# First stage of a four-layer kernel: context values for 128 tokens at a time, by way of DRAM

## The chip, the cores and the metric

The kernel runs on one core of one Trainium2 chip, as one program. The metric is the time of one execution in device microseconds; a kernel's time is the median of several runs. Five engines work side by side, each through its own queue in order: TensorE (PE; its weight loads are shown as PEld), VectorE (DVE), ScalarE (ACT), GpSimd (POOL) and SyncE (SP), which here issues most DMAs.

## What is computed

The input is x (16 batches of 256 tokens, 256 wide) and a context of 16 x 77 tokens, 256 wide. Four layers add to x in turn, each scaled by the tanh of a gate: an attention of x over context and x together, a mixture of experts, a second cross-attention, a gated linear attention. Only the first one is touched:

```python
x = layer_norm(image_embeds, ln1_g, ln1_b)      # the context, 77 tokens a batch
l = layer_norm(latents, ln2_g, ln2_b)           # the latents (x, normed once before), 256 tokens a batch
q = l @ Wq                                      # 16 heads of 64
kv = jnp.concatenate([x, l], axis=1) @ Wkv      # 333 tokens a batch
k, v = jnp.split(kv, 2, axis=-1)
w = softmax(q k^T / 8)                          # per head, 256 x 333
out = (w v) @ Wo
```

## The kernel before

Everything is float32; in the records each matmul appears as two. The whole first stage is `stage0_fast`. Its engines run in the order in which the code names their instructions (`Pinned`, line 50, so nearly all records bear L50). The work is cut into 64 units, one for each batch b and group g of four heads. A unit runs, on TensorE: the scores of (b, g), then denominators and outputs of the unit before it (`values`), then at g = 1 the transposes of the next batch (`turn`) and the projection of the last one, at g = 2 the values of the next batch (`all_values`), and then queries and keys of the next unit (`heads`).

A batch has 256 tokens of its own and 77 of its context, 333 together. `turn` transposes xn (256 tokens) and cn (77 tokens) into one PSUM pair; VectorE scales them into kvT (128 partitions x 2 x 333), the context behind the tokens. `all_values` cuts the 333 columns into three chunks of KC = 111, and makes values for each chunk with 2 halves of 512 x 2 steps of contraction. ACT copies one half of the result into v, VectorE the other. `heads` makes q (256 columns) and k (333 columns) for two heads at a time; ACT scales q, VectorE copies k.

`scores` has six slots of 111 keys (two pairs of heads x three chunks) by two heads x 256 queries, in three PSUM pairs; ACT takes the exponential of each pair into e. `sums` adds the three chunks on GpSimd into es, and es into esum (a check on the size of the sums). `values` turns es into denominators by a matmul with ones, and e with v into outputs; in the last unit it takes the denominators straight from e (`last`). es and e have two buffers each, oT and cn one. The PSUM pool has four pairs of banks.

Context rows are loaded two batches ahead by SP (`load_c`, line 110), three buffers of 77 rows. At n = 1 SP issues `clear_rows`, 16 writes of 640 KB that clear the experts' rows in DRAM; before them stand all loads of weights and of x.

Of the kernel before, what the change touches and what calls it, by code (L numbers as in the profile page):

```python
# [10 lines left out]
F32 = mybir.dt.float32  # L11
# [6 lines left out]
P = 128  # L18
# [55 lines left out]
def layers(ctx: ExitStack, tc: tile.TileContext, t, out, check):  # L74
# [30 lines left out]
    w12 = s12.enter_context(tc.tile_pool(name="s12w", bufs=1, side="right"))  # L105
    ws1 = s1.enter_context(tc.tile_pool(name="s1w", bufs=1, side="right"))
    if fast:
        ctxs = s0.enter_context(tc.tile_pool(name="f0c", bufs=3))

    def load_c(b):  # L110
        cs[b] = ctxs.tile([S2, D], F32, tag="c", name="c")
        nc.sync.dma_start(out=cs[b], in_=t["ctx"][b])

    vec = const("vec", [P, V_N])
    nc.sync.dma_start(out=vec, in_=t["vec"])
# [16 lines left out]
    nc.sync.dma_start(out=prio, in_=t["prio"])  # L132
    wq2, wk2, wv2, wo2 = (load_w(n, D, D, w12) for n in ("wq2", "wk2", "wv2", "wo2"))
    if fast:
        both, own, pmask = (w12.tile(shape, F32, tag=n, name=n) for n, shape in (
            ("both", [P, 2, D]), ("own", [P, 2, 32]), ("pmask", [P, 2])))
        before, offs = (ws1.tile(shape, F32, tag=n, name=n) for n, shape in (
            ("before", [P, P]), ("offs", [P, 2, 2, 8])))

        gbo = const("gbo", [P, D])  # L140
        for n, x in (("both", both), ("own", own), ("pmask", pmask), ("before", before),
                     ("offs", offs)):
# [390 lines left out]
    def stage0_fast():  # L533
        with ExitStack() as sx:
# [5 lines left out]
            def pair(name):  # L540
                return pairs.tile([P, 2, 512], F32, tag="ps", name=name)
# [3 lines left out]

            esum, rsum = check["esum"], check["rsum0"]

            xn, cn, kvT, v, oT = {}, {}, {}, {}, {}

            y, mvs, tallies = {}, {}, []  # L550

            def norm_c(b):
                mvs[b, "c"] = moments(cs[b].unsqueeze(1), S2, 1)

            def norm_x(b):
                mvs[b, "x"] = moments(xs[b])
# [7 lines left out]

            def normed_all(b):
                xn[b] = w1.tile([P, 2, D], F32, tag="xn", name="xn")
                cn[b] = w1.tile([S2, 1, D], F32, tag="cn", name="cn")
                normed(xn[b], y.pop(b), *mvs.pop((b, "y")))
                normed(cn[b], cs[b].unsqueeze(1), *mvs.pop((b, "c")), S2, 1)

            def turn(b):
                kvT[b] = w2.tile([P, 2, NK], F32, tag="kvT", name="kvT")
                both = pair("tr")
                for k in range(2):
                    ps = both[:, k, :]
                    for i in range(2):
                        pe.transpose(ps[:, i * P:(i + 1) * P], xn[b][:, i, k * P:(k + 1) * P], ident)
                    pe.transpose(ps[:, S:NK], cn[b][:, 0, k * P:(k + 1) * P], ident[:S2, :S2])
                for k in range(2):
                    ps = both[:, k, :]  # L580
                    dve.tensor_scalar(kvT[b][:, k, :S], ps[:, :S], vec[:, V_LN2G + k:V_LN2G + k + 1],
                                            vec[:, V_LN2B + k:V_LN2B + k + 1], ALU.mult, ALU.add)
                    dve.tensor_scalar(kvT[b][:, k, S:], ps[:, S:NK], vec[:, V_LN1G + k:V_LN1G + k + 1],
                                            vec[:, V_LN1B + k:V_LN1B + k + 1], ALU.mult, ALU.add)

            def all_values(b, *between):
                v[b] = w2.tile([KC, 3, 1024], F32, tag="v", name="v")
                for c in range(3):
                    both = pair("v")
                    for h in range(2):  # L590
                        ps = both[:, h, :]
                        for k in range(2):
                            pe.matmul(ps[:KC, :], kvT[b][:, k, c * KC:(c + 1) * KC],
                                             wkv0[:, k, 1024 + h * 512:1024 + (h + 1) * 512],
                                             start=k == 0, stop=k == 1)
                    act.copy(v[b][:, c, :512], both[:KC, 0, :])
                    dve.tensor_copy(v[b][:, c, 512:], both[:KC, 1, :])
                    for x in between[c:c + 1]:
                        x()

            qk = {}

# [14 lines left out]
            def scores(b, g):  # L617

                x_qk = qk.pop((b, g))
                e = w2.tile([KC, 6, 2, S], F32, tag="e", name="e")  # L620
                for u in range(0, 6, 2):
                    sc = pair("sc").rearrange("p j (x s) -> p j x s", x=2)
                    for x in range(2):
                        n, c = divmod(u + x, 3)
                        for j in range(2):
                            r = slice(64 * j, 64 * j + 64)
                            pe.matmul(sc[:KC, j, x, :], x_qk[r, n, S + c * KC:S + (c + 1) * KC],
                                             x_qk[r, n, :S], start=True, stop=True)
                    act.activation(e[:, u:u + 2], sc[:KC].rearrange("p j x s -> p x j s"), AF.Exp)
                return b, g, e  # L630

            def sums(b, g, e):
                es = w2.tile([KC, 2, 2 * S], F32, tag="es", name="es")
                by_chunk = e.rearrange("p (n c) j s -> p n c (j s)", n=2)
                pool.tensor_tensor(es, by_chunk[:, :, 0], by_chunk[:, :, 1], ALU.add)
                pool.tensor_tensor(es, es, by_chunk[:, :, 2], ALU.add)
                for n in range(2):
                    pool.tensor_tensor(esum[:KC], esum[:KC], es[:, n, :], ALU.add)
                return b, g, e, es

            def values(b, g, e, es, last=False):
# [7 lines left out]
                for c in range(3 if last else 1):  # L649
                    for h, r in heads:  # L650
                        n, j = divmod(h, 2)
                        x = e[:, 3 * n + c, j, :] if last else es[:, n, j * S:(j + 1) * S]
                        pe.matmul(den[r, :S], ones[:KC, :32], x, start=c == 0, stop=not last or c == 2)
                for i in range(2):
                    for c in range(3):
                        for h, r in heads:
                            n, j = divmod(h, 2)
                            lo = (4 * g + h) * 64 + 32 * i
                            pe.matmul(ps[r, i * S:(i + 1) * S], v[b][:, c, lo:lo + 32], e[:, 3 * n + c, j, :],
                                      start=c == 0, stop=c == 2)  # L660
# [52 lines left out]
            for n, (b, g) in enumerate(units):  # L713
# [16 lines left out]
                    clear_rows()  # L730
                now = sums(*now)
                if behind is not None:
                    values(*behind)
                if g == 1 and b + 1 < B:
                    turn(b + 1)
                if g == 1 and b > 0:
# [15 lines left out]

            run(ahead_of, B, 0)
            run(behind_scores, B, 0)
            values(*behind, last=True)
            tally()
            run(ahead_of, B, 1)
            run(behind_scores, B, 1)
# [241 lines left out]
    def stage1_fast(keep, prep, bank):  # L1000
        with ExitStack() as sx:
# [6 lines left out]
            def own_bank(name):  # L1008
                return psx.tile([P, 512], F32, tag="ps", name=name)

            dve.tensor_scalar(gbo, both[:, 1, :], gate[:, 2:3], None, ALU.mult)
# [40 lines left out]
            def context(b):  # L1052

                if b % 4 == 0:
                    context_keys(b // 4)
                ps, cT = bank("v"), cTs[b // 4][:, :, b % 4, :]
                for k in range(2):
                    pe.matmul(ps[:S2, :D], cT[:, k, :], wv2[:, k, :], start=k == 0, stop=k == 1)
                vc = keep.tile([S2, D], F32, tag=f"vc{b}", name=f"vc{b}")
                dve.tensor_tensor(vc, ps[:S2, :D], both[:S2, 0, :], ALU.add)  # L1060
                ctx_side[b] = negs[b], kds[b // 4][:, :, :, b % 4 * S2:(b % 4 + 1) * S2], vc


# [960 lines left out]
def _arrays(i):  # L2024
# [4 lines left out]
    def cols(v):  # L2029
# [31 lines left out]
        "both": np.broadcast_to(np.stack([f["L1_xattn_wv_b"], f["L1_xattn_wo_b"]]), (P, 2, D)),  # L2061
# [29 lines left out]
```

## Time and profile before

| | |
|---|---|
| three runs | 1917.66, 1918.72, 1922.24 us; median 1918.72 |
| the profiled execution | 1917.57 us, span 1915.7 us, granted clock 0.995 |
| TensorE, 112 to 966 us (first stage) | busy 852.77 of 854.00 |
| VectorE, ScalarE, GpSimd there | 433.17, 350.90, 517.56 |
| DMA there | 3% of the 16 DMA engines' time, 10 GB/s |
| values, TensorE records | 384 of 128x512, weights 128*111 |
| copies of values | ACT 48 x 586 ns, VectorE 48 x 691 ns |
| exponentials | 192 x 1021 ns |
| GpSimd sums | 64 x 2363, 64 x 2351, 128 x 1274 ns |

A row of the profile names the engine, the operation, output<-inputs by the program's names, and the shapes; 128*111 means 128 rows of contraction and 111 columns of weights. "Idle before" is the engine's idle time before the instruction and what ended it. Matmul durations overlap, so the spacing of a series is read from the chain or from the start times.

### The profile page before, as it was taken

The numbers are of one execution on the slowest core, as the hardware profiler recorded it, in microseconds if no ns is written. First come the engines' busy times: TensorE is split into PE (matmuls) and PEld (weight loads), VectorE is DVE, ScalarE is ACT, GpSimd is POOL, SyncE is SP. The second block draws the span as 40 slices with busy tenths as digits, with TensorE's granted clock in tenths as the row PEclk, the third lists the DMA queues.
The fourth block names the chain that finished last, engine by engine and source line by source line (L and its number), as shares of the span: only waits on it lengthen the run. The fifth ranks groups of instructions, "written<-read, shape, count | busy, mean of one in ns | idle before, by whom it ended". The sixth has DMA issues, their size and how long they took to land.

```text
span 1915.7 us, 34858 instructions
## 1 busy us (share of the span) xinstructions
PE 1886.3 (98%) x13960; PEld 1311.6 (68%) x13960; DVE 1096.9 (57%) x2667; ACT 871.1 (45%) x1790; POOL 991.6 (52%) x891
## 2 busy tenths in 40 slices
PE   8999999999999999999999899999999999999997
PEld 5666666666666666666787766667777777777775
DVE  3334555455554555545464388876666666666654
ACT  3333344343343433434343478744444444454452
POOL 3644756557565575655634656314444444444433
PEclk9999999999999999999999999999999999999999
DMA  9400000000000000000068823000000000000000
GB/s 332 148 1 3 14 11 14 7 11 14 11 14 7 11 14 9 12 7 9 12 220 253 224 43 49 15 1 7 6 7 7 6 12 7 6 7 7 12 7 14
DMA packets 54107, 75.16 MB, mean 39 GB/s; under 512 B 10112, under 2 KB 43760, under 8 KB 53424
## 3 DMA queue, kind: packets, MB, share of 16 engines
q1 hardware_dynamic: 41648, 56.05, 8.7%
q0 software_dynamic: 12288, 16.79, 4.3%
q8 instruction: 112, 1.84, 0.4%
q14 instruction: 59, 0.48, 0.1%
HBM read 39.27 MB, written 33.55 MB: 38 GB/s over the span
## 4 chain that ended last, share of the span: by engine, by line
PE 95%; DVE 2%; ACT 1%; POOL 0%; DMA 0%; issue 0%; SPq 0%; ACTq 0%; POOLq 0%; DVEq 0%
PE o L50 13%; PE qk L50 13%; PE sc L50 10%; PE v L50 9%; PE proj L50 7%; PE kq L1548 6%; PE sc L1548 5%; PE ex L50 3%; PE gq L1548 3%; PE v L1548 3%; PE proj L1548 3%; PE o L1548 3%; PE gz L1548 2%; PE den L1548 2%; PE low L1548 1%; PE ms L1548 1%
## 5 line engine op out<-in xcount | busy, mean ns | idle before, releaser
L50 POOL TENSOR_SCALAR rs<-mv 128x2 f32<-128x2 f32 (+1 forms) x91 | 17.5, 192 | 458.7 <-DVE mv L50 455.1
L50 ACT ACTIVATE qk<-qk 128x256 f32<-128x256 f32 x128 | 49.3, 385 | 343.6 <-PE qk L50 343.5
L50 ACT ACTIVATE e<-sc 111x1024 f32<-111x1024 f32 x192 | 182.3, 1021 | 16.9 <-PE sc L50 16.9
L50 PE MATMUL sc<-qk 64*111 64x256 f32 x1536 | 182.2, 383 | 0.0
L50 PE MATMUL o<-e,v 111*32 111x256 f32 x3072 | 177.5, 379 | 0.0
L50 PE MATMUL v<-wkv,kvT 128*111 128x512 f32 x384 | 169.1, 597 | 0.6 <-DVE kvT L50 0.6
L50 DVE RECIPROCAL rd<-o 128x256 f32<-128x256 f32 x64 | 112.3, 1755 | 99.7 <-PE o L50 99.7
L50 PEld LDWEIGHTS sc<-qk 64*111 64x111 f32 x1536 | 132.1, 172 | 52.9 <-issue 29.0
L50 POOL TENSOR_TENSOR esum<-esum,es 111x512 f32<-111x512 f32 x128 | 163.1, 1274 | 10.0
L50 PE MATMUL qk<-kvT,wkv 128*128 128x333 f32 x512 | 164.3, 443 | 0.0
L50 POOL TENSOR_TENSOR es<-e 111x1024 f32<-111x1024 f32 x64 | 151.2, 2363 | 23.9 <-ACT e L50 22.7
L50 POOL TENSOR_TENSOR es<-es,e 111x1024 f32<-111x1024 f32 x64 | 150.4, 2351 | 5.0
L50 PEld LDWEIGHTS o<-e,v 111*32 111x32 f32 x3072 | 99.8, 110 | 66.0
L50 POOL TENSOR_TENSOR k<-e,ee 128x256 f32<-128x256 f32 x64 | 46.8, 731 | 189.4 <-ACT e L50 189.4
L50 DVE COPY qk<-qk 128x333 f32<-128x333 f32 x128 | 64.5, 504 | 124.5 <-ACT qk L50 123.0
L50 PE MATMUL qk<-kvT,wq 128*128 128x256 f32 x512 | 134.3, 385 | 0.0
L50 PEld LDWEIGHTS v<-wkv,kvT 128*111 128x111 f32 x384 | 67.0, 177 | 91.3 <-issue 89.9
L50 POOL TENSOR_TENSOR at<-at,at 128x768 f32<-128x768 f32 x63 | 113.9, 1807 | 24.4 <-DVE at L50 24.4
L50 DVE TENSOR_TENSOR at<-sc,amask 128x768 f32<-128x768 f32 x64 | 61.3, 957 | 113.8 <-PE sc L1548 110.2
L50 POOL DMA_INDIRECT x<-rows_out,pos x64 | 100.4, 1568 | 36.5 <-issue 15.7
L50 PEld LDWEIGHTS qk<-kvT,wkv 128*128 128x128 f32 x512 | 97.2, 190 | 30.0
L50 PEld LDWEIGHTS qk<-kvT,wq 128*128 128x128 f32 x512 | 94.3, 189 | 34.0 <-issue 13.2
(247 smaller groups left out, 4113.7 us busy)
## 6 DMA issues: line engine op xcount, KB each, us to landing
rows<-zero SPq DMA_DIRECT2D x16, 640.0 KB
xin<-rows SPq DMA_DIRECT2D x16, 640.0 KB
rows_out<-y SPq DMA_DIRECT2D x16, 384.0 KB
x<-in_x_dram SPq DMA_DIRECT2D x16, 256.0 KB
rows_out<-y SPq DMA_DIRECT2D x16, 256.0 KB
out_dram<-x SPq DMA_DIRECT2D x15, 256.0 KB
wkv<-in_wkv_dram SPq DMA_DIRECT2D x2, 1024.0 KB
ew<-in_ew_dram SPq DMA_DIRECT2D x2, 1024.0 KB
```

The lines of the kernel that those rows point to most:

```text
L50: x = getattr(self.engine, name)(*a, **k)
L1548: tc.keep_in_program_order(nc.tensor.matmul(*a, **k))
```

## The change

The 16 x 77 = 1232 context tokens are taken as one list and cut into ten groups of 128 (the last of 80). Each group is loaded, normed and transposed once, at the batch in which it begins (batches 0, 1, 3, 4, 6, 8, 9, 11, 13, 14). Its transposes go to a tile ctxT, from which ACT copies each batch's columns into kvT. Its values are made once, copied to a tile vc, and written to one DRAM tile for each batch (vctx); each batch from 1 on reads its 77 rows back into the third chunk of v. Batch 0 gets its rows from PSUM directly. A batch's own tokens give two chunks of 128 values.

The slots of a unit are therefore 128, 128 and 77 keys. The scores go through PSUM in the order (0, 1), (2, 5), (3, 4), so that the two context slots share a pair. es has one buffer. esum takes all 128 partitions. The denominators of the first unit, too, are taken straight from e. The two biases of the third layer come as two tiles (bv, and gbo directly) in place of one (both). Keys are still made for 333 columns in each batch.

```diff
-        ctxs = s0.enter_context(tc.tile_pool(name="f0c", bufs=3))
+        ctxs = s0.enter_context(tc.tile_pool(name="f0c", bufs=2))
+    c_rows = B * S2
+    c_new = {b: j for j in range(-(-c_rows // P)) for b in [P * j // S2]}
+    def c_count(j):
+        return min(P, c_rows - P * j)
+    def c_pieces(b):
+        lo, hi = b * S2, (b + 1) * S2
+        return [(j, max(lo, P * j) - P * j, max(lo, P * j) - lo, min(hi, P * j + P) - max(lo, P * j))
+                for j in range(lo // P, (hi - 1) // P + 1)]
...
             def turn(b):
...
-                    pe.transpose(ps[:, S:NK], cn[b][:, 0, k * P:(k + 1) * P], ident[:S2, :S2])
+                    if n:
+                        pe.transpose(ps[:, S:S + n], cn[b][:n, 0, k * P:(k + 1) * P], ident[:n, :n])
...
-                    dve.tensor_scalar(kvT[b][:, k, S:], ps[:, S:NK], ...)
+                    if n:
+                        dve.tensor_scalar(ctxT[j][:, k, :n], ps[:, S:S + n], ...)
+                for j, at, to, n in c_pieces(b):
+                    act.copy(kvT[b][:, :, S + to:S + to + n], ctxT[j][:, :, at:at + n])
+            def some_values(x, n):
+                both = pair("v")
+                for h in range(2):
+                    for k in range(2):
+                        pe.matmul(both[:n, h, :], x[:, k, :], wkv0[:, k, 1024 + h * 512:1024 + (h + 1) * 512],
+                                         start=k == 0, stop=k == 1)
+                return both
+            def copied(to, both, n):
+                act.copy(to[:n, :512], both[:n, 0, :])
+                dve.tensor_copy(to[:n, 512:], both[:n, 1, :])
             def all_values(b, *between):
...
+                if b in c_new:
+                    j = c_new[b]
+                    n = c_count(j)
+                    both = some_values(ctxT[j][:, :, :n], n)
+                    vc = w1.tile([P, 1024], F32, tag="vc", name="vc")
+                    copied(vc, both, n)
+                    if b == 0:
+                        copied(v[b][:, 2, :], both, S2)
+                    for to in range(1, B):
+                        for jj, at, row, n in c_pieces(to):
+                            if jj == j:
+                                nc.sync.dma_start(out=vctx[to][row:row + n], in_=vc[at:at + n, :])
+                if b > 0:
+                    nc.sync.dma_start(out=v[b][:S2, 2, :], in_=vctx[b])
+                for c in range(2):
+                    copied(v[b][:, c, :], some_values(kvT[b][:, :, chunks[c]], P), P)
+                    if between:
+                        between.pop(0)()
+                for x in between:
+                    x()
...
-                for u in range(0, 6, 2):
+                for slot in ((0, 1), (2, 5), (3, 4)):
...
-                es = w2.tile([KC, 2, 2 * S], F32, tag="es", name="es")
+                es = w1.tile([P, 2, 2 * S], F32, tag="es", name="es")
...
-                pool.tensor_tensor(es, es, by_chunk[:, :, 2], ALU.add)
+                pool.tensor_tensor(es[:S2], es[:S2], by_chunk[:S2, :, 2], ALU.add)
...
-                    values(*behind)
+                    values(*behind, by_chunk=n == 1)
```

More of the change, by code (lines that the diff above doesn't have):

```diff
@@ L107, in layers @@
     if fast:
-        ctxs = s0.enter_context(tc.tile_pool(name="f0c", bufs=3))
+        ctxs = s0.enter_context(tc.tile_pool(name="f0c", bufs=2))
[7 more added lines that the diff above has]
+                for j in range(lo // P, (hi - 1) // P + 1)]
     def load_c(b):
-        cs[b] = ctxs.tile([S2, D], F32, tag="c", name="c")
-        nc.sync.dma_start(out=cs[b], in_=t["ctx"][b])
+        if b in c_new:
+            j, n = c_new[b], c_count(c_new[b])
+            cs[b] = ctxs.tile([P, D], F32, tag="c", name="c")
+            nc.sync.dma_start(out=cs[b][:n], in_=t["ctx"].rearrange("b s d -> (b s) d")[P * j:P * j + n])
     vec = const("vec", [P, V_N])
@@ L134, in layers @@
     if fast:
-        both, own, pmask = (w12.tile(shape, F32, tag=n, name=n) for n, shape in (
-            ("both", [P, 2, D]), ("own", [P, 2, 32]), ("pmask", [P, 2])))
+        bv, own, pmask = (w12.tile(shape, F32, tag=n, name=n) for n, shape in (
+            ("bv", [P, D]), ("own", [P, 2, 32]), ("pmask", [P, 2])))
         before, offs = (ws1.tile(shape, F32, tag=n, name=n) for n, shape in (
@@ L140, in layers @@
         gbo = const("gbo", [P, D])
-        for n, x in (("both", both), ("own", own), ("pmask", pmask), ("before", before),
+        for n, x in (("bv", bv), ("bo", gbo), ("own", own), ("pmask", pmask), ("before", before),
                      ("offs", offs)):
@@ L546, in stage0_fast @@
             esum, rsum = check["esum"], check["rsum0"]
-            xn, cn, kvT, v, oT = {}, {}, {}, {}, {}
+            xn, cn, kvT, v, oT, ctxT = {}, {}, {}, {}, {}, {}
+            vctx = [tc.dram_tile([S2, 1024], F32, name=f"vctx{b}") for b in range(B)]
+            chunks = [slice(0, P), slice(P, S), slice(S, NK)]
+            counts = [P, P, S2]
             y, mvs, tallies = {}, {}, []
             def norm_c(b):
-                mvs[b, "c"] = moments(cs[b].unsqueeze(1), S2, 1)
+                if b in c_new:
+                    n = c_count(c_new[b])
+                    mvs[b, "c"] = moments(cs[b][:n].unsqueeze(1), n, 1)
             def norm_x(b):
@@ L566, in normed_all @@
                 xn[b] = w1.tile([P, 2, D], F32, tag="xn", name="xn")
-                cn[b] = w1.tile([S2, 1, D], F32, tag="cn", name="cn")
                 normed(xn[b], y.pop(b), *mvs.pop((b, "y")))
-                normed(cn[b], cs[b].unsqueeze(1), *mvs.pop((b, "c")), S2, 1)
+                if b in c_new:
+                    n = c_count(c_new[b])
+                    cn[b] = w1.tile([P, 1, D], F32, tag="cn", name="cn")
+                    normed(cn[b][:n], cs[b][:n].unsqueeze(1), *mvs.pop((b, "c")), n, 1)
             def turn(b):
@@ L573, in turn @@
                 both = pair("tr")
+                j = c_new.get(b)
+                n = 0 if j is None else c_count(j)
                 for k in range(2):
@@ L577, in turn @@
                         pe.transpose(ps[:, i * P:(i + 1) * P], xn[b][:, i, k * P:(k + 1) * P], ident)
-                    pe.transpose(ps[:, S:NK], cn[b][:, 0, k * P:(k + 1) * P], ident[:S2, :S2])
+                    if n:
+                        pe.transpose(ps[:, S:S + n], cn[b][:n, 0, k * P:(k + 1) * P], ident[:n, :n])
+                if n:
+                    ctxT[j] = w2.tile([P, 2, P], F32, tag="ctxT", name="ctxT")
                 for k in range(2):
@@ L582, in turn @@
                                             vec[:, V_LN2B + k:V_LN2B + k + 1], ALU.mult, ALU.add)
-                    dve.tensor_scalar(kvT[b][:, k, S:], ps[:, S:NK], vec[:, V_LN1G + k:V_LN1G + k + 1],
-                                            vec[:, V_LN1B + k:V_LN1B + k + 1], ALU.mult, ALU.add)
-            def all_values(b, *between):
[L587 to L599, printed above, removed]
+                    if n:
+                        dve.tensor_scalar(ctxT[j][:, k, :n], ps[:, S:S + n], vec[:, V_LN1G + k:V_LN1G + k + 1],
+                                                vec[:, V_LN1B + k:V_LN1B + k + 1], ALU.mult, ALU.add)
@@ new lines, in all_values @@
+            def all_values(b, *between):
+                v[b] = w2.tile([P, 3, 1024], F32, tag="v", name="v")
+                between = list(between)
+                if b in c_new:
+                    j = c_new[b]
[17 more added lines that the diff above has]
+                    x()
@@ L619, in scores, with values @@
                 x_qk = qk.pop((b, g))
-                e = w2.tile([KC, 6, 2, S], F32, tag="e", name="e")
-                for u in range(0, 6, 2):
+                e = w2.tile([P, 6, 2, S], F32, tag="e", name="e")
+                for slot in ((0, 1), (2, 5), (3, 4)):
                     sc = pair("sc").rearrange("p j (x s) -> p j x s", x=2)
-                    for x in range(2):
-                        n, c = divmod(u + x, 3)
+                    rows = counts[slot[0] % 3]
+                    for x, u in enumerate(slot):
+                        n, c = divmod(u, 3)
                         for j in range(2):
                             r = slice(64 * j, 64 * j + 64)
-                            pe.matmul(sc[:KC, j, x, :], x_qk[r, n, S + c * KC:S + (c + 1) * KC],
+                            pe.matmul(sc[:rows, j, x, :], x_qk[r, n, S + chunks[c].start:S + chunks[c].stop],
                                              x_qk[r, n, :S], start=True, stop=True)
-                    act.activation(e[:, u:u + 2], sc[:KC].rearrange("p j x s -> p x j s"), AF.Exp)
+                    act.activation(e[:rows, slot[0]:slot[1] + 1:slot[1] - slot[0]],
+                                   sc[:rows].rearrange("p j x s -> p x j s"), AF.Exp)
                 return b, g, e
             def sums(b, g, e):
-                es = w2.tile([KC, 2, 2 * S], F32, tag="es", name="es")
+                es = w1.tile([P, 2, 2 * S], F32, tag="es", name="es")
                 by_chunk = e.rearrange("p (n c) j s -> p n c (j s)", n=2)
                 pool.tensor_tensor(es, by_chunk[:, :, 0], by_chunk[:, :, 1], ALU.add)
-                pool.tensor_tensor(es, es, by_chunk[:, :, 2], ALU.add)
+                pool.tensor_tensor(es[:S2], es[:S2], by_chunk[:S2, :, 2], ALU.add)
                 for n in range(2):
-                    pool.tensor_tensor(esum[:KC], esum[:KC], es[:, n, :], ALU.add)
+                    pool.tensor_tensor(esum, esum, es[:, n, :], ALU.add)
                 return b, g, e, es
-            def values(b, g, e, es, last=False):
+            def values(b, g, e, es, by_chunk=False):
                 if g == 0:
@@ L647, in values @@
                 heads = [(h, slice(32 * h, 32 * h + 32)) for h in range(4)]
-                for c in range(3 if last else 1):
+                for c in range(3 if by_chunk else 1):
                     for h, r in heads:
                         n, j = divmod(h, 2)
-                        x = e[:, 3 * n + c, j, :] if last else es[:, n, j * S:(j + 1) * S]
-                        pe.matmul(den[r, :S], ones[:KC, :32], x, start=c == 0, stop=not last or c == 2)
+                        rows = counts[c]
+                        x = e[:rows, 3 * n + c, j, :] if by_chunk else es[:, n, j * S:(j + 1) * S]
+                        pe.matmul(den[r, :S], ones[:rows, :32], x, start=c == 0, stop=not by_chunk or c == 2)
                 for i in range(2):
@@ L658, in values @@
                             lo = (4 * g + h) * 64 + 32 * i
-                            pe.matmul(ps[r, i * S:(i + 1) * S], v[b][:, c, lo:lo + 32], e[:, 3 * n + c, j, :],
+                            rows = counts[c]
+                            pe.matmul(ps[r, i * S:(i + 1) * S], v[b][:rows, c, lo:lo + 32], e[:rows, 3 * n + c, j, :],
                                       start=c == 0, stop=c == 2)
@@ L754, in stage0_fast @@
             run(behind_scores, B, 0)
-            values(*behind, last=True)
+            values(*behind, by_chunk=True)
             tally()
@@ L1009, in own_bank @@
                 return psx.tile([P, 512], F32, tag="ps", name=name)
-            dve.tensor_scalar(gbo, both[:, 1, :], gate[:, 2:3], None, ALU.mult)
+            dve.tensor_scalar(gbo, gbo, gate[:, 2:3], None, ALU.mult)
             kb = w1.tile([P, 2, 2], F32, tag="kb", name="kb")
@@ L1059, in context @@
                 vc = keep.tile([S2, D], F32, tag=f"vc{b}", name=f"vc{b}")
-                dve.tensor_tensor(vc, ps[:S2, :D], both[:S2, 0, :], ALU.add)
+                dve.tensor_tensor(vc, ps[:S2, :D], bv[:S2], ALU.add)
                 ctx_side[b] = negs[b], kds[b // 4][:, :, :, b % 4 * S2:(b % 4 + 1) * S2], vc
@@ L2060, in _arrays @@
         "own": np.broadcast_to(own, (P, 2, 32)).astype(np.float32),
-        "both": np.broadcast_to(np.stack([f["L1_xattn_wv_b"], f["L1_xattn_wo_b"]]), (P, 2, D)),
+        "bv": np.broadcast_to(f["L1_xattn_wv_b"], (P, D)), "bo": np.broadcast_to(f["L1_xattn_wo_b"], (P, D)),
         "x": f["x"], "ctx": f["ctx_1024"], "fside": f["fside_BxSxS2_0"], "mask": f["mask_BxSxS2_ik1"], "vec": vec,
```

## The prediction

> **What bounds the kernel now.** I read the page's busy rows and its chain first, then the chain of waits of one batch of the first stage, then the weight loads, and last the few places where the change adds a wait.
>
> ```profile
> PE 1886.3 (98%) x13960; PEld 1311.6 (68%) x13960; DVE 1096.9 (57%) x2667; ACT 871.1 (45%) x1790; POOL 991.6 (52%) x891
> PE 95%; DVE 2%; ACT 1%; POOL 0%; DMA 0%; issue 0%; SPq 0%; ACTq 0%; POOLq 0%; DVEq 0%
> ```
>
> TensorE is busy 98% of the span and 95% of the chain that ended last; in the first stage from 112 to 966 us it is busy 852.77 of 854.00. So a matmul less there is time less, unless another engine then falls behind. The chain in order of time (start, us, what) for the batch from 472 us:
>
> ```profile
> 472.06 0.48 PE rtr L50 x4
> 472.54 10.30 PE v L50 x24
> 500.58 3.16 PE o L50 x56
> 513.85 0.73 PE tr L50 x6
> ```
>
> A batch repeats every 59.9 us. Its values take 24 matmul records (12 matmuls, two records each) in 10.30 us, 0.429 us a record. Four transposes of rxn take 0.48, six of xn and cn 0.73, so a context transpose is worth about 0.125.
>
> **Values, the term that decides.** Before, each batch makes 12 matmuls for values (three chunks of 111 tokens, two halves, two steps of contraction), 192 in all. After, a batch makes 8 for its own 256 tokens, and the 1232 context tokens make 10 groups of up to 128 with 4 each: 128 + 40 = 168. That is 24 matmuls or 48 records less: 48 x 0.429 = 20.6 us. Batches 2, 5, 7, 10, 12 and 15 (those in which no group begins) drop from 24 to 16 records each; the others stay at 24. What could spoil it is that the weights grow from 111 to 128 columns. The weight loads of these matmuls (the timeline), and the last stage's values, which have 128 columns and the same 512 moved (the chain):
>
> ```profile
> 472.81 0.18 PEld L50 LDWEIGHTS v<-wkv,kvT 128*111 128x111 f32 x1 [0.25 <-issue]
> ```
> ```profile
> 1303.31 3.44 PE v L1548 x8
> ```
>
> A load takes 0.18 and then 0.25 passes before the next one issues; with 128 columns the spacing is 3.44/8 = 0.430, the same. So I take 0.429 also after the change. A rule of the Trainium skill speaks against it: "TensorE: Matmul & The Clock Gate", section "LDWEIGHTS (loading the stationary operand)", says that a load costs by its columns and not by its contraction, and the section "Back-to-back issue gap" that loads and matmuls together set the spacing. By column counts alone nothing would be saved, since 3 x 111 and 128 + 128 + 77 are both 333, and the sum would stay near 1916; the 0.25 us of idle between loads decides for the matmuls.
>
> **Scores, denominators, outputs.** The same number of matmuls with 256 columns moved. Weights of 111 columns (load 172 ns on 64 rows) become two of 128 (186 ns in the last stage's sc<-q,k) and one of 77 (no row at 64 rows; 147 ns at 128 rows): mean (2 x 186 + 147)/3 = 173. The last stage's sc with 128 columns runs 8 records in 0.88 to 0.92 us, 0.11 each; here 24 take 2.78, 0.116. I take nothing. Contraction over 128 or 77 rows in place of 111 streams the same 256 columns: nothing. The exponentials keep 1024 elements a partition (1.02 us), POOL's sums keep their elements (2.36 and 1.27).
>
> **Context transposes.** 32 become 20 (two for each group): 12 x 0.125 = 1.5 us less. The remaining ones are 128 wide like rtr's, 0.12 each, so not dearer.
>
> **The single buffer of chunk sums.** POOL's first addition of a unit now also waits until TensorE has finished the denominators of the unit before; behind it in POOL's queue stand the other sums and the scatters, and TensorE's next denominators wait for it. The tightest unit I find (timelines of POOL and TensorE):
>
> ```profile
> 503.94 2.35 POOL L50 TENSOR_TENSOR es<-e 111x1024 f32<-111x1024 f32 x1 [0.77 <-ACT e L50]
> 506.37 2.35 POOL L50 TENSOR_TENSOR es<-es,e 111x1024 f32<-111x1024 f32 x1
> ```
> ```profile
> 500.51 0.64 PE L50 MATMUL o<-es,ones 111*32 111x256 f32 x8
> 510.62 0.64 PE L50 MATMUL o<-es,ones 111*32 111x256 f32 x8
> ```
>
> The buffer would be free at 501.15, and POOL starts at 503.94 because the last exponential comes then: 2.8 us before it binds. The sums end at 508.72 and are due at 510.62: another 1.9. Cost nothing, because scores always stand ahead of denominators on TensorE and the exponentials end later than both; without that cover it would be what the first rival prices.
>
> **Context values by DRAM.** 24 writes and 15 reads join SP's queue, about 4.7 MB each way, while context loads fall from 16 to 10. Issuing and landing of a 256 KB load took 2.73 us (the x load at the start) and a rows_out write 2.56, so write and read with three or four issues of 0.4 are near 7 us. A group's values end 3.4 us into the batch's 10.30, its copies (ACT 0.59, DVE 0.69) 1.3 later: 477.3 in the batch shown, landed by about 484.5, and first needed at 510.7 as weights of batch 8's first outputs: 26 us of slack. At the start the cover is thinner: SP issues the clearing of the expert rows from 36.93 to 60.42 and the writes queue behind it, so batch 1 has its values at about 67, needed at 90.4. Behind the waiting DMAs on SP stand only context loads, two batches ahead. Cost nothing; were the cover gone, each microsecond late costs 15 us, once a batch.
>
> **Copies of the context slots.** ACT gets 26 copies from ctxT to kvT. They are short (rows from 128x16 at 0.17 to 77x256 at 0.37; I take 0.25), but the copy of a new group waits for VectorE and the scaling of the queries stands behind it:
>
> ```profile
> 522.17 1.52 DVE L50 TENSOR_SCALAR kvT<-tr,vec 128x256 f32<-128x256 f32 x4
> 523.61 0.74 DVE L50 SCALAR_TENSOR_TENSOR x<-proj,gate,x 128x512 f32<-128x512 f32 x1
> 524.27 0.49 DVE L50 COPY qk<-qk 128x333 f32<-128x333 f32 x1
> ```
> ```profile
> 525.43 2.85 PE L50 MATMUL sc<-qk 64*111 64x256 f32 x24
> ```
>
> VectorE gets there late because oT waits for the projection. Four operations become 1.62 (128 wide is 0.40 by the 0.35 and 0.54 of 77 and 256), to 523.79; ACT's copy to 524.05, the scaling (0.38) to 524.43, VectorE's copy to 524.95, scores due at 525.43. Nothing, with 0.5 to spare; by the dearer ends perhaps 0.3 in nine batches, 2.7 us. Batches without a group lose two VectorE operations here. ACT's and VectorE's value copies fall from 48 to 43 each, hidden.
>
> **The start.** The first values wait for two more VectorE results: +0.2. The unit with n = 1 takes its denominators straight from e: 72 records for 56. The last unit runs 72 in 4.07 against 3.16, so +0.9, but a wait goes:
>
> ```profile
> 38.71 0.64 PE L50 MATMUL o<-es,ones 111*32 111x256 f32 x8 [1.80 <-POOL es L50]
> ```
>
> That is 0.95 earlier. Next late there are the scores at 46.62, which have no projection to hide the new ACT copy: VectorE's kvT would end at 45.1, copy and scaling at 45.75, VectorE's copy at 46.28, so 0.3 of the 0.95 remains and the 0.2 eats it. I take 0, bounds -1.0 and +0.6.
>
> **Handover to the second stage.** In the built order four of the first eight xT transposes now also wait for the last residual on VectorE (973.50 + 0.75 = 974.25; now they end at 974.34). I take +0.3, between 0 and 0.6. The orders of all engines behind that are the same but for a few loads.
>
> **Sum.** -20.6 - 1.5 + 0 + 0.3 = -21.8 us. The profiled execution took 1917.57 (span 1915.70 and 1.87 around it): 1895.8. The median of the three runs, 1918.72, is 1.15 above it; I add half, 1896.4.
>
> **Rivals.** (1) Slower: POOL becomes the pace through the single buffer. For it: POOL is 61% busy in the stage (517.56 of 854). It decides once the sums end more than 1.9 us later than now; then each 0.45 us a unit costs 62 x 0.45 = 28 us and ends at 1924. Against: the free 2.8 us ahead of it. (2) The way through DRAM is late: it decides beyond 26 us; at 1 us over, 15 us come back, 1911; at 2, 1926. Against: the 2.7 us landings. (3) The change doesn't do what it says, since loads pace TensorE: only transposes go, 1916. Against: the 0.430 row.
>
> **How the numbers follow.** Forecast 0.86, rival 1 0.05, rival 2 0.05 (0.03 of it still faster, 0.01 and 0.01), rival 3 0.04. About 0.3% (5.8 us) is what a measurement can tell here. Faster 0.86 + 0.03 = 0.89, same 0.04 + 0.01 = 0.05, slower 0.05 + 0.01 = 0.06. The range goes down to 1893 (the start's -1.0, no handover, the fast end of runs) and up to 1902 (slot copies 2.7, start and handover 0.9, the rest of the median's offset 0.6, and the near edge of rival 2).
>
> **What would show it.** Right: v records 336 in place of 384 at 0.43 spacing, batch periods of 59.9 and 56.3 us in turn, cn transposes gone from six batches, TensorE idle before o near zero. Wrong: an idle of TensorE put down to v's DMA, to POOL es or to qk, v's spacing above 0.44, or a last projection of the first stage that ends after 955 us (now 973.3, so 951 to 952 is expected).

## The result and the profile after

The changed kernel takes 1900.66 us, the median of four runs (1893.98 to 1903.45), against 1919.65 for the kernel before beside it: ratio 0.9895, 95% interval 0.9867 to 0.9924. (A ratio is that of runs taken side by side, with disturbed ones left out, so it need not be the quotient of two medians.) The forecast was 1896.4, between 1893 and 1902. The profiled execution took 1900.88, span 1899.1, granted clock 0.993.

The page's busy row and its chain, to be held against the two rows at the head of the prediction:

```profile
PE 1872.1 (99%) x13916; PEld 1310.1 (69%) x13916; DVE 1085.0 (57%) x2632; ACT 867.4 (46%) x1804; POOL 986.0 (52%) x879
...
PE 95%; DVE 2%; ACT 1%; DMA 0%; issue 0%; POOL 0%; SPq 0%; DVEq 0%; POOLq 0%; ACTq 0%
```

TensorE has lost 14.2 us of busy time and the span 16.6. It is still 95% of the chain, so nothing took its place as the bound. From the chain in order of time (start, us, what), over three batches, of which a group begins in the first two and none in the third; the transposes are those of the batch that follows:

```profile
462.76 10.30 PE v L50 x24
...
500.96 3.17 PE o L50 x56
504.13 0.80 PE tr L50 x6
...
564.17 0.59 PE tr L50 x4
...
582.63 6.87 PE v L50 x16
```

The same 24 records of values still take 10.30, as before the change with 111 columns of weights; where only 16 are left they take 6.87. Both are 0.429 a record. The weight loads of the short series (the timeline, idle before in brackets):

```profile
582.90 0.19 PEld L50 LDWEIGHTS v<-wkv,kvT 128*128 128x128 f32 x1 [0.24 <-issue]
583.33 0.19 PEld L50 LDWEIGHTS v<-wkv,kvT 128*128 128x128 f32 x1 [0.24 <-issue]
```

A load grew from 0.18 to 0.19 and the idle behind it shrank from 0.25 to 0.24: the wider weights were paid out of idle time. The waits of TensorE that bear on the first stage and its end (total us, times, longest):

```profile
PE rtr L50 <- ACT rxn L50: 1.2, 2, 1.0
PE v L50 <- DVE ctxT L50: 1.0, 1, 1.0
...
PE sc L50 <- DVE qk L50: 0.5, 1, 0.5
PE xT L50 <- DVE x L50: 0.4, 1, 0.4
```

No row names v's DMA, and none names POOL's es, whose 1.8 us stood there before. The wait for qk comes once, in the first batch.

The table compares executions by stage. "Batch 1" is the start of batch 1's first value matmul, "middle" the time from there to the end of the stage's last projection, all in us, read from TensorE's timelines.

| kernel | batch 1 | middle | projection ends |
|---|---|---|---|
| before | 52.55 | 920.91 | 973.46 |
| changed | 51.19 | 902.46 | 953.65 |
| changed, `e1_again` | 54.09 | 902.46 | 956.55 |
| changed, `e8_changed_once_more` | 54.13 | 902.46 | 956.59 |
| `e2_pad_values` | 52.85 | 921.36 | 974.21 |
| `e3_slots_alone` | 51.67 | 922.22 | 973.89 |
| `e4_es_alone` | 51.80 | 922.56 | 974.36 |
| `e10_wait_for_sums` | 53.95 | 900.76 | 954.71 |
| `e7_stats_first` | 51.28 | 899.17 | 950.45 |
| `e9_stats_first_more` | 53.79 | 899.17 | 952.96 |

The middle is the same to the hundredth in three executions of the changed kernel; what differs from run to run is the start, and places behind the first stage.

### The profile page after: what moved, and what is told of

The parts are those of the page before. It is cut to its first block, busy times and chain, and to the rows that moved or that the text cites. A ratio compares the mean times of both kernels' runs of the same rounds, so it can differ in the third digit from the quotient of the medians.

```text
span 1899.1 us, 34899 instructions
## 1 busy us (share of the span) xinstructions
PE 1872.1 (99%) x13916; PEld 1310.1 (69%) x13916; DVE 1085.0 (57%) x2632; ACT 867.4 (46%) x1804; POOL 986.0 (52%) x879
## 4 chain that ended last, share of the span: by engine, by line
PE 95%; DVE 2%; ACT 1%; DMA 0%; issue 0%; POOL 0%; SPq 0%; DVEq 0%; POOLq 0%; ACTq 0%
PE o L50 14%; PE qk L50 13%; PE sc L50 11%; PE v L50 8%; PE proj L50 7%; PE kq L1607 6%; PE sc L1607 5%; PE gq L1607 3%; PE ex L50 3%; PE v L1607 3%; PE proj L1607 3%; PE o L1607 3%; PE gz L1607 2%; PE den L1607 2%; PE low L1607 1%; PE ms L1607 1%
## 5 line engine op out<-in xcount | busy, mean ns | idle before, releaser
L50 ACT ACTIVATE e<-sc 128x1024 f32<-128x1024 f32 (+1 forms) x192 | 181.6, 1016 | 18.1 <-PE sc L50 18.1
L50 PE MATMUL sc<-qk 64*128 64x256 f32 (+1 forms) x1536 | 183.1, 384 | 0.5 <-DVE qk L50 0.5
L50 PE MATMUL o<-e,v 128*32 128x256 f32 (+1 forms) x3072 | 177.9, 379 | 0.0
L50 PEld LDWEIGHTS sc<-qk 64*128 64x128 f32 (+1 forms) x1536 | 132.0, 172 | 55.4 <-issue 27.6
L50 POOL TENSOR_TENSOR esum<-esum,es 128x512 f32<-128x512 f32 x128 | 162.4, 1269 | 10.0
L50 POOL TENSOR_TENSOR es<-e 128x1024 f32<-128x1024 f32 x64 | 151.2, 2362 | 27.0 <-ACT e L50 24.3
L50 POOL TENSOR_TENSOR es<-es,e 77x1024 f32<-77x1024 f32 x64 | 150.1, 2346 | 5.0
L50 PEld LDWEIGHTS o<-e,v 128*32 128x32 f32 (+1 forms) x3072 | 99.8, 110 | 66.3
L50 PE MATMUL proj<-wo0h,oT 128*128 128x256 f32 x512 | 113.5, 380 | 0.0
L50 PE MATMUL v<-wkv,kvT 128*128 128x512 f32 x256 | 112.5, 592 | 0.0
```

Source lines behind the costliest of these rows:

```text
L50: x = getattr(self.engine, name)(*a, **k)
```

## The experiments

The theory: the gain is the 24 value matmuls that are no longer made, and the rest of the change is near zero because it lies beside TensorE's work.

**The changed kernel twice more** (no edit). The first asks whether the 5 us by which the profiled execution stayed behind the sum belong to the change.

> The changed kernel once more, for a second trace. Theory: what the forecast missed, 3.3 us of the profiled execution, is mostly two stretches of lower granted clock (1.6 us in batch 3's values, 2.1 us at the start of the last stage). In another execution they lie elsewhere or are absent: span 1895 to 1901, ratio 0.988 to 0.991, and the chain of the first stage the same to 0.1 us apart from such stretches. Rival: they belong to the change, at the same places with the same sizes.

Measured: median 1899.68, ratio 0.9894 (0.9871 to 0.9917). The low-clock stretches that I describe further down came back in the same places, which spoke for the rival that they belong to the change. The second repeat was made beside `e9_stats_first_more`:

> The changed kernel beside the next one on the same chip. Median 1898 to 1902.

Measured: 1898.28, ratio 0.9886 (0.9866 to 0.9905). Here the stretch at the start of the last stage is gone, so that rival falls for it.

**The values put back.** Six batches make one more chunk of values, so that each batch has 24 records again.

```diff
                 for x in between:
                     x()
+                if b not in c_new:
+                    some_values(kvT[b][:, :, chunks[1]], P)
```

> The changed kernel, and in the six batches in which no group begins four more value matmuls (eight records) whose result is not used. Theory: the saved value matmuls are the whole gain, so the time goes back by 48 x 0.429 = 20.6 us, to the time before or up to 2 us above it (ratio 0.999 to 1.002). Rival: the gain comes from less copying or from other parts, and ACT and VectorE have fewer copies here still: ratio stays below 0.995.

Measured: 1916.74, ratio 1.0 (0.9982 to 1.0017). In the chain, the values of a batch in which no group begins:

```profile
592.40 0.48 PE rtr L50 x4
592.89 10.30 PE v L50 x24
```

The 6.87 are 10.30 again, the middle is back at 921.36, and the gain is gone, although the DRAM path, the slots and the single buffer are all still there. That places the gain. It rules out the rival of this run (fewer copies, or other parts) and the prediction's third, and it leaves the other parts together a net cost of at most some 3 us, the width of the interval to either side.

**The slots alone**, in the kernel before: chunks of 128, 128 and 77, the order (0, 1), (2, 5), (3, 4), and every batch with its own context values.

```diff
-                v[b] = w2.tile([KC, 3, 1024], F32, tag="v", name="v")
+                v[b] = w2.tile([P, 3, 1024], F32, tag="v", name="v")
...
-                            pe.matmul(ps[:KC, :], kvT[b][:, k, c * KC:(c + 1) * KC],
+                            pe.matmul(ps[:KC, :], kvT[b][:, k, chunks[c]],
...
-                for u in range(0, 6, 2):
+                for slot in ((0, 1), (2, 5), (3, 4)):
```

> The kernel before with chunks of 128, 128 and 77 keys, each batch making its own context values (192 matmuls as before), no DRAM, es with two buffers. Theory: nothing but the 0.02 us a unit by which scores and outputs were longer in the changed kernel, about +1.2 us: ratio 0.999 to 1.002. Rival, loads pace TensorE: columns are the same in sum, so the same ratio; but then the values' 8 records with 77 columns would be shorter than those with 128. The theory has all 24 at 0.429.

Measured: 1919.83, ratio 1.0006 (0.9991 to 1.002). A batch became 60.01 instead of 59.92, 0.02 a unit, and the middle 1.3 longer than before. That is too little for the timing to show, but the trace shows it.

**One buffer of es alone**, in the kernel before, with the first unit's denominators straight from e.

```diff
-                es = w2.tile([KC, 2, 2 * S], F32, tag="es", name="es")
+                es = w1.tile([KC, 2, 2 * S], F32, tag="es", name="es")
...
-                    values(*behind)
+                    values(*behind, last=n == 1)
```

> The kernel before with one es buffer and the denominators of the first unit straight from e, nothing else changed. Theory: the 1.8 us wait of TensorE for POOL's first sums goes, 0.95 us are won there and partly lost again; the single buffer costs nothing: -1.0 to 0 us, ratio 0.998 to 1.001, TensorE never idle before o in the first stage. Rival, POOL becomes the pace: TensorE idle before o in many units, over +5 us.

Measured: 1918.52, ratio 0.9995 (0.998 to 1.0009). The batch period behind the first three is 59.92, as with two buffers, and TensorE's waits have no row of o for POOL's es. GpSimd did not become the pace. The 0.95 us expected of the first unit are there: from the end of the first values to batch 1's it takes 28.48, and 29.50 in the kernel before. The middle is 1.65 longer, 1.3 of it through a low-clock stretch in batch 3's values (11.60 instead of 10.30), in a kernel that has no DRAM path.

**The read from DRAM later.** The read of a batch's context values is taken out of `all_values` and issued in the batch itself, behind a short GpSimd write to the same rows of v which ties it to that place. First one unit before the values are used (g == 0), then in the unit in which they are used (g == 1):

```diff
-                if b > 0:
-                    nc.sync.dma_start(out=v[b][:S2, 2, :], in_=vctx[b])
...
+                if g == 0 and b > 0:
+                    pool.memset(v[b][:S2, 2, 0:1], 0.0)
+                    nc.sync.dma_start(out=v[b][:S2, 2, :], in_=vctx[b])
                 now = sums(*now)
```

> The changed kernel, but each batch's context values are read back from DRAM only in unit g = 0 of their batch: GpSimd clears one column of the tile there, which the read must wait for. GpSimd reaches it at about 503 us in the batch that needs its values at 510.7 (times of the trace before). Theory: a read takes near 3 us, so it lands some 4 us before it is needed: same time as the changed kernel, ratio to before 0.988 to 0.992. Rival, the way through DRAM is a tight one: TensorE waits for v's DMA, over +15 us.

Measured: 1900.3, ratio 0.9902 (0.9882 to 0.9922), and no wait for v's DMA. So at least a unit of the slack was real.

> As the one before, but the column is cleared in unit g = 1, after GpSimd's sums of g = 0, at about 511.5 us against a need at 510.7. Theory: TensorE waits there in each of 15 batches for clearing and read, 3 to 4 us each, so 45 to 60 us over the changed kernel: 1945 to 1960 us, with the wait put down to v's DMA. It prices what the distance hides. If it costs under 20 us, the read is faster or the need later than I reckoned.

Measured: 1975.81, ratio 1.0304 (1.0287 to 1.0321). TensorE's wait, one of the fifteen on TensorE's timeline, SP's issue for it, and the windows behind it (the stretch, its length, then busy us and instructions of PE, PEld, DVE, ACT and POOL, the granted clock, the DMA share and GB/s):

```profile
PE o L50 <- DMA v<-vctx: 48.4, 15, 4.2
```
```profile
539.29 3.11 PE L50 MATMUL o<-e,v 77*32 77x256 f32 x32 [3.87 <-DMA v<-vctx]
```
```profile
535.94 0.28 SPq L790 DMA_DIRECT2D v<-vctx  x1
```
```profile
539.00:545.00 6.00, 5.71 (x45) 4.09 (x46) 3.42 (x2) 0.00 (x0) 4.17 (x3) 0.72 0.01 3
545.00:560.00 15.00, 15.00 (x118) 11.36 (x120) 6.32 (x25) 4.80 (x10) 1.65 (x3) 1.00 0.00 1
```

The read takes 3.35 us from issue to use (539.29 - 535.94). The wait is 48.4 in all, but the kernel lost 75.5 against `e5_read_one_unit_before` on the same chip: in the 6 us behind the wait shown the granted clock is 0.72 on the average before it is back at 1.00. Over the two profiled executions the granted clock is 0.980 of 1974.0 us and 0.993 of 1904.9, so 39.5 and 13.3 us of clock were not granted; the 26 us between them are about what the waits leave unexplained (75.5 - 48.4 = 27.1). I had expected 45 to 60. The second rival's mechanism exists, its price is half as high again as its wait, and the changed kernel stays clear of it.

**The first unit waits for the sums again** (one execution):

```diff
-                    values(*behind, by_chunk=n == 1)
+                    values(*behind)
```

> The changed kernel, with the denominators of the first unit from es again. Theory: TensorE waits 1.8 us for POOL there and makes 16 records less (0.9), so the first values of the second batch start about 0.9 us later than in the changed kernel, less what the scores' wait for VectorE (0.5) takes up: 0.4 to 0.9.

Measured: 1895.71, with the old wait back:

```profile
PE o L50 <- POOL es L50: 1.8, 1, 1.8
```

Batch 1's values begin at 53.95, inside the 51.19 to 54.13 of the changed kernel's three executions, which differ by more than the 0.4 to 0.9 in dispute. But they differ in when the first values begin and how long these take (10.40, 12.88 and 12.78, here 12.10). From the end of the first values to batch 1's, all three executions of the changed kernel take 29.11 and this one 30.10: taking the denominators by chunk is worth 0.99 here, a little more than expected. This execution has no low-clock stretch in batch 3, with the same wait ahead of it, and its middle is 1.7 shorter than the changed kernel's.

**The router's statistics first.** VectorE's small product rs in batch 2 takes 2.31 us instead of 0.16 and holds up TensorE, in both kernels (next sections). The edit exchanges two entries, so that it comes earlier in the unit:

```diff
-                        2: [(route.weigh, -2), (route.stats, -1)], 3: [...]
+                        2: [(route.stats, -1), (route.weigh, -2)], 3: [...]
```

> The changed kernel with the router's statistics ahead of the router's weights in unit g = 2 (two lines of the order exchanged). Theory: VectorE's 0.16 us operation rs took 2.3 us in batch 2 because GpSimd's first sum (2.36 us) started 0.1 us before it; run 1 us earlier it meets an idle GpSimd, takes 0.16, and TensorE's wait of 1.2 us before rtr goes, and with it the low clock behind it (1.6): -1.2 to -3 us against the changed kernel, batch period 56.6 in place of 58.3. Rival: rs waits for something else: 2.3 us again.

Measured: 1896.07, ratio 0.989 (0.9871 to 0.9908). TensorE no longer waits for rxn there, and batch 2's period falls from 58.27 to 56.61. The second time, beside a run of the changed kernel:

> The router's statistics first, once more, beside the changed kernel. Theory: 1.6 us less in every execution (batch 2's period 56.6 in place of 58.3) and 1.6 us more in those where the clock would have fallen behind it: median 1.5 to 4 us below the changed kernel. Rival: the difference of the run before was chance, within 1 us of each other.

Measured: 1894.37, ratio 0.9861 (0.9839 to 0.9884), 3.9 below `e8_changed_once_more` on the same chip. The middle is 899.17 both times, 3.3 less than the changed kernel's: 1.66 at the wait (1.2 of it idle), 1.6 by the stretch of low clock, which neither execution has. Only the first part is there against every execution: `e10_wait_for_sums` has the wait without the stretch, and its middle of 900.76 is 1.6 above. The intervals of the ratios overlap, so by the times alone the step is likely and not settled; by the traces the 1.6 us are there.

## Why the prediction was right, and where it was off

**Values: right.** Forecast -20.6 by 48 records at 0.429. A batch with 16 records repeats every 56.61 and one before every 59.92: 3.31, and six of them make 19.9, with everything else that changed in a batch inside; the values alone take 6.87 instead of 10.30, six times 3.43, which is 20.6. The records are 256 and 80, 336. Read by column counts alone, the rule that I weighed ("TensorE: Matmul & The Clock Gate" of the Trainium skill, "LDWEIGHTS (loading the stationary operand)" with "Back-to-back issue gap") would have left 1916; the measured spacing of 0.429 at 128 columns decides against that reading of it in this case.

**Context transposes: mis-sized.** Forecast -1.5, measured about -0.2. I priced a transpose at 0.125 from the difference between six in 0.73 and four of rxn in 0.48. The four that remain take 0.59, not 0.48, and six with the wider cn take 0.80, not 0.73: 9 x 0.07 - 6 x 0.14 = -0.2. So two things were wrong, of about 0.6 us each: the row of rxn was not the row of the same thing (its four stand behind other work than the four of xn; why that takes less is not shown), and the wider transposes are dearer, which I had denied. The short batches repeat every 56.61 and not every 56.3.

**Scores and outputs: mis-sized.** Forecast nothing; they went from 2.78 to 2.79 and from 3.16 to 3.17, 0.02 a unit, about +1.2 over 62 units. `e3_slots_alone` shows this part by itself. The projection gave some back (6.95 to 6.91, 15 times, -0.6).

**DRAM path, single buffer, slot copies: right.** Their costs were zero, as the waits show. With the 3.35 us of `e6_read_in_the_unit` for each, the reads land 16.5 us or more before TensorE needs them, by this estimate; the thinnest cover is batch 1's, issued at 70.15 and needed at 90.0. ScalarE's new copies are 25, where the prediction counted 26. The tightest step that I found, in the batch from 462 us, on ScalarE, VectorE and TensorE:

```profile
514.15 0.20 ACT L50 COPY kvT<-ctxT 128x4 f32<-128x4 f32 x1 [11.81 <-DVE ctxT L50]
514.25 0.38 ACT L50 ACTIVATE qk<-qk 128x256 f32<-128x256 f32 x1
```
```profile
513.71 0.41 DVE L50 TENSOR_SCALAR ctxT<-tr,vec 128x128 f32<-128x128 f32 x1
...
514.69 0.50 DVE L50 COPY qk<-qk 128x333 f32<-128x333 f32 x1
```
```profile
515.74 2.86 PE L50 MATMUL sc<-qk 64*128 64x256 f32 x24
```

ScalarE's idle time before the copy (11.81) ends with VectorE's ctxT, as foreseen; then copy, scaling and VectorE's copy follow each other and end at 515.19, 0.55 before the scores start. The prediction said 0.5.

**The start: the middle was right, the spread was not.** Forecast 0, between -1.0 and +0.6; the three executions of the changed kernel have -1.4, +1.5 and +1.6 against before's one. The weight loads of the first values show it (changed kernel, then `e8_changed_once_more`):

```profile
14.36 0.19 PEld L50 LDWEIGHTS v<-wkv,ctxT 128*128 128x128 f32 x1 [0.24 <-issue]
```
```profile
14.11 0.34 PEld L50 LDWEIGHTS v<-wkv,ctxT 128*128 128x128 f32 x1 [0.52 <-issue]
```

The load is nearly twice as long, and with the idle behind it the spacing is 0.86 instead of 0.43. In `e8_changed_once_more` this lasts until 17.3, in the changed kernel's first execution the values are 0.43 apart from 12.2 on. The column of the granted clock reads 1.00 in both, so it does not show this; that TensorE's pace was halved is read from the spacing. The kernel before has a slow stretch in its first values as well, and there the column does show it (columns as above):

```profile
10.81:14.22 3.41, 3.05 (x4) 1.32 (x5) 1.29 (x4) 0.00 (x0) 0.00 (x0) 0.50 1.04 370
```

Its first values take 11.88, those of the changed kernel's first execution 10.40, so the -1.4 is luck. What is left without these values is 11.17 ahead of them and 29.50 behind in the kernel before, 11.68 and 29.11 in the changed one: +0.1, which is the forecast's 0. I had bounded the start by waits alone. The last projection's limit of 955 that the prediction set was passed in two of three executions (956.55, 956.59), whose first values begin 0.4 and 0.6 later and take 2.5 and 2.4 longer; their middle is 902.46 like the first's. Two more of the signs named for being wrong appear, and neither touches the gain: TensorE's wait for qk (0.5, once, in the first batch, where the prediction had put the new copy in the way), and a spacing of values above 0.44, in the first values of two executions and in batch 3, both from a slower pace of TensorE.

**Handover: the wait came, its cost is not clear.** Forecast +0.3. The new wait of xT for x is there (0.4); the end of the experts' matmuls comes 117.76 behind the last projection in the changed kernel's first execution, 117.06 and 117.07 in the others, and 117.02 before: +0.7, 0 and 0. Two of three show no cost, and what the 0.7 of the first is stays open.

**The 5 us between sum and profiled execution.** The sum gives -21.8, the spans -16.6. Transposes +1.3, scores and outputs less projection +0.6, start -1.4, handover +0.4 and the tail behind TensorE's last matmul +0.5 (8.86 against 8.33) make 1.4. The other 3.7 are two stretches of low clock, seen in the windows of the changed kernel (columns as above):

```profile
164.51:167.93 3.42, 2.21 (x28) 1.34 (x21) 3.42 (x2) 1.16 (x3) 3.34 (x2) 1.00 0.00 0
167.93:171.34 3.41, 3.41 (x7) 1.46 (x5) 0.86 (x2) 0.59 (x1) 3.25 (x3) 0.50 0.00 0
...
1251.00:1256.00 5.00, 4.84 (x24) 3.52 (x22) 4.73 (x9) 2.10 (x6) 1.61 (x3) 0.74 0.00 0
1256.00:1261.00 5.00, 5.00 (x15) 4.09 (x15) 1.02 (x4) 0.12 (x1) 1.42 (x2) 0.58 0.01 3
```

The first makes batch 3's values 11.90 instead of 10.30 (+1.6); the second puts the last stage's second series of values 43.55 behind the first instead of 41.47 (+2.1). In `e8_changed_once_more` the second place has its full clock:

```profile
1256.00:1261.00 5.00, 3.94 (x22) 2.82 (x23) 4.92 (x9) 2.21 (x6) 1.51 (x3) 1.00 0.00 0
```

The batch-3 stretch is not a cost of the DRAM path: it occurs without that path (`e4_es_alone`) and is missing with it (`e2_pad_values`, `e10_wait_for_sums`). The traces show what goes with it. Within one execution the low stretches begin whole multiples of 3.41 us apart (167.93, 1079.29 and 1253.37 in the changed kernel, 267 and 51 times 3.413) and last 3.41 us or a multiple of it, unless the end cuts them off. The two windows of 3.41 us that hold batch 2's wait in `e10_wait_for_sums`, to be held against the first two above:

```profile
166.05:169.47 3.42, 2.77 (x48) 1.57 (x38) 2.59 (x2) 0.56 (x2) 3.26 (x4) 1.00 0.00 0
169.47:172.88 3.41, 2.84 (x9) 1.48 (x10) 2.07 (x2) 1.50 (x4) 3.33 (x2) 1.00 0.00 0
```

In the changed kernel's first execution TensorE is idle for 1.21 us of one such period (3.42 - 2.21) and has half the clock in the next; in `e10_wait_for_sums` the same wait is split into 0.65 and 0.57, and the clock stays. So it goes in all ten executions that have this wait: where 1.20 or 1.21 us of it fall in one period the stretch follows (the changed kernel three times, `e4_es_alone`, `e5_read_one_unit_before`), where it is 1.04 or less it does not (the kernel before, `e2_pad_values`, `e3_slots_alone`, `e6_read_in_the_unit`, `e10_wait_for_sums`). Where the periods lie differs from execution to execution, so by these ten it is chance, in either kernel, whether the stretch comes. No edit tested this, and idle time alone is no rule for other places: the 1.8 us wait of `e10_wait_for_sums` lies whole in one period (36.35 to 39.77), and no low stretch follows. Where batch 2's wait is gone (`e7_stats_first`, `e9_stats_first_more`) the stretch was not seen either.

Over all repeats the medians gained 19.0, 19.0 and 22.1 (1919.65 to 1900.66, 1918.72 to 1899.68, 1920.39 to 1898.28), where the forecast had 22.3.

## What to carry to other kernels

Where one engine holds 95% of the chain, count its instructions per batch and price them by the spacing of the same instruction in the trace: here that one product was the gain, and everything else only had to be shown to be hidden. Price a removed instruction by a series of the same kind in the same place, and the ones that stay by their new width: the difference between two unlike series (0.73 - 0.48) promised 0.25 a batch where 0.14 was saved, and the wider transposes that stayed cost 0.6 us of it again. A wait of the bounding engine can cost more than its own length, since the clock may stay low behind it: 48.4 us of waits cost 75.

## What the runs showed of the hardware that was not expected

**A small VectorE operation lasts as long as GpSimd's addition.** On VectorE and GpSimd in the changed kernel:

```profile
164.12 2.31 DVE L50 SCALAR_TENSOR_TENSOR rs<-mv,rs 128x2 f32<-128x2 f32 x1 [1.10 <-POOL rs L50]
```
```profile
164.05 2.37 POOL L50 TENSOR_TENSOR es<-e 128x1024 f32<-128x1024 f32 x1
```

Two elements a partition take 2.31 us, and both end at the same time (166.43 and 166.42). In `e7_stats_first` it comes first:

```profile
163.00 0.15 DVE L50 SCALAR_TENSOR_TENSOR rs<-mv,rs 128x2 f32<-128x2 f32 x1
```
```profile
163.76 2.37 POOL L50 TENSOR_TENSOR es<-e 128x1024 f32<-128x1024 f32 x1 [1.18 <-ACT e L50]
```

The Trainium skill has a rule for it: "SBUF — State Buffer", section "Who interferes with whom", says that the two engines share one pair of SBUF ports under an exclusive lock, and that a VectorE instruction with two SBUF inputs, as this one has in mv and rs, contends with a GpSimd instruction that reads SBUF. The equal ends agree with that, and so does the 0.15 when VectorE is first. A second case in the changed kernel's trace fits as well: at 34.05 the same product begins 1.14 us into such an addition, takes 1.23 and ends within 0.02 us of it, while the others of its kind in the first stage, none of which has such an addition beside it for 0.1 us, take 0.15 to 0.16. In the kernel before the same pair ends at 171.20 and 171.19 (168.89 + 2.31, 168.82 + 2.37), so this is no part of the difference between the two; it is what the two exchanged entries removed.

**A short wait can be followed by a longer stretch of low clock**: 3.87 us of waiting by a granted clock of 0.72 over 6 us in `e6_read_in_the_unit`, and 1.2 us by 3.41 us at 0.50 in batch 3 of the changed kernel. Whether it comes went, for that wait, with where the wait lay between marks 3.41 us apart, and not with its length: the same wait, split by such a mark, was followed by full clock.
